# Layer 2's row ends with features on partitions and layer 3's weights centred beforehand

## The chip, the cores and the metric

The kernel runs on one core of one Trainium2 chip. The metric is the time of one execution in microseconds (us); the time before is 1886.3 us, the median of 4 runs (1885.71 to 1888.77). Engines are named as in the profile: PE is TensorE (PEld its weight loads), DVE is VectorE, ACT is ScalarE, POOL is GpSimd, SP is SyncE, whose queue issues most loads.

## The reference, cut to what matters

Four graph layers run over the same 2708 x 256 matrix `x` and the same 2708 x 2708 matrix `adj`. Each layer's output is added to its input and the rows are normalised. What the change touches is the end of layer 2 and the products that layer 3 begins with:

```python
# layer 2: GRU cells on 256 features; dn = de = diagonal of adj
y = dn[:, None] * (edge_output + node_output)          # layer 2's result
x = layernorm(x + y)                                   # (v - mean(v)) / sqrt(var(v) + 1e-5) by rows
# layer 3
h = x @ neigh_W.T
h = adj @ h / (adj.sum(axis=1, keepdims=True) + 1.0)
z = concatenate([x, h], axis=-1) @ lin_W.T
x = layernorm(x + z)
```

`neigh_W` is 256 x 256 and `lin_W` is 256 x 512. Since `adj @` acts from the left, the kernel uses `z = x @ A + (adj @ (x @ B)) / degree`, with A the first half of `lin_W.T` and B = `neigh_W.T` times its second half. A and B side by side, 256 x 512, are `lwn` in the code. So a finished row of layer 2 is needed for two products: `x @ A`, which is added to the row and kept in `y3_d` until layer 3 ends that row, and `x @ B`, the row of `h3` that layer 3 multiplies with `adj`.

## The kernel before, in words

Rows are cut into 22 tiles of 128 (the last has 20), `NT = 22`; 256 features are two chunks of 128 (`FC = 2`). A tile of rows can lie in memory with rows on partitions or, transposed, with features on partitions.

**Layer 0 and its preparation (to about 250 us).** While PE multiplies strips of `adj` with `x`, the weights of layer 3 are prepared in the pool `prep`: `lw` (`lin_W.T`) and `nw` are loaded by SP's queue, A is stored to `lwn_d` by POOL (L548), `nw` is transposed (L554), B is multiplied (L559), copied out by ACT (L562) and stored by POOL (L563). `lwn_d` is read back into `lwn` at the start of layer 2 (L373). In the same stage DVE picks out `diag`, the diagonal of `adj`, as a 128 x 22 table with rows on partitions (L458).

**Layer 1 (250 to 610 us) and the statistics of layer 2 (to some 720 us)** follow. At the end of the latter, small tables are transposed by PE (L966), copied by ACT (L970) and stored by POOL to `st_d` (L976).

**Layer 2's main loop (from about 890 us, L1247).** The 2708 columns are covered by three units, each with two halves of 512, 512 and 330 columns. For each unit and each of three heads, eleven steps run. One step loads blocks of `adj` by SP's queue (L264), builds two tiles `p` with two ACT instructions and one DVE product each (L1258 to L1262), makes four sums of them on DVE (L304 to L307), and issues seven PE products (`seven`, L317; a 32-bit product appears twice in the profile, so 14 there, a transpose once) into seven PSUM banks: `m1` takes one, `m26`, `m75` and `m43` two each. The eighth PSUM bank is `bank()`, a pool with a single buffer. Whoever takes it waits until what it held before has been read out.

**What is put between.** Everything else of layer 2 runs in slots between those products: `seven` calls `between()` after its third and its sixth product (`slots` = (2, 5); in the first unit of layer 3, after each product for some of the steps), and each call runs the next piece, up to a `yield`, of a generator from the lists `urgent` and `later`. `urgent` has `project` (L1098). `later` has `node(u, est)` of the unit before: for each half, the GRU cell (`cell`, L1115, products at L1128), whose result `yt` has features on partitions; the addition of the edge cell's result `et` (L1217); then the row ends. Layer 3 needs `h3` of all rows and so waits for the last unit's row ends (`while urgent or later: between()`, L1331).

**The row ends.** `by_tiles` (L1191) cuts a half into row tiles; a tile that lies in two halves is put together by POOL (L1201) and ended when its second part is there. Each tile takes three slots:

- `node_rows` (L1152): PE transposes the two chunks of `yt` into `bank` (L1157). DVE multiplies them by the rows' `diag` and adds the residual `xs[t]` (L1160). Then `layernorm` (L178): `bn_stats` (L170), `bn_aggr` (L172) and an addition (L174) on DVE, the power -0.5 on POOL (L175), and the normalisation on DVE (L181).
- `rows_turned` (L1166): PE transposes the normalised row back (L1170), ACT copies it out of `bank` (L1172).
- `rows_end` (L1175): PE multiplies its two chunks with `lwn` into one bank of 512 columns (L1179, four products of 512 columns in the profile). ACT copies the right half to `h3` (L1180), DVE adds the left half to the row (L1181), POOL stores the row to `y3_d` (L1182).

The loop in `node` (L1220) sets these apart: in step i it does `node_rows` of tile i, `rows_end` of tile i-2, `rows_turned` of tile i-1.

**What sets the order.** The program's order gives priorities; a scheduler in the compiler, which works with durations of its own, orders the instructions of each engine, and each engine then runs its own in that order and waits at the head of its queue. Buffers of a pool are reused when all who used them are done; `nleft` keeps one buffer of most tags (`xt2` and `et` for a cell's inputs, `yt` for its result), so the next half's inputs are loaded by POOL's queue (`load_cell`, L1184) when the cell before has let go of them.

The last function that the diff touches, for rows of `adj` with negative entries (`layer2_signed`, behind a branch that isn't taken with this data), ends its rows by `layer2_end` (L218).

## Time and profile before

| what | before |
| --- | --- |
| median of 4 runs | 1886.3 us (1885.71 to 1888.77) |
| the profiled execution | 1889.28 us |
| its span, first to last instruction | 1887.2 us |
| PE busy, instructions | 1843.2 us (98%), 7561 |
| DVE busy | 1279.8 us (68%), 2280 |
| ACT busy | 689.9 us (37%), 1419 |
| POOL busy | 254.9 us (14%), 419 |
| granted TensorE clock, mean | 0.996 |
| row ends of the first unit (two halves) | 1216 to 1291 and 1326 to 1375 us |
| row ends of the second unit | 1482 to 1525 and 1567 to 1609 us |
| row ends of the third unit | 1674 to 1692 and 1717 to 1741 us |

Busy time is summed over an engine's instructions; matmuls are pipelined, so their durations overlap and a busy PE isn't PE at its peak. A line of the timeline has start and length in us, engine, line of the kernel, operation, what is written and read, shapes and count; brackets at the end tell how long the engine had been idle and what ended that.

### The profile page before, as it was taken

To read this page: it belongs to the slowest core of one execution; us is meant where nothing else is said; L and a number is where in the kernel's file an instruction comes from. 1 tells how busy PE (TensorE), PEld (TensorE's weight loads), DVE (VectorE), ACT (ScalarE), POOL (GpSimd) and SP (SyncE) were. 2 spreads that over 40 slices of the span, in tenths; PEclk is the share of its full clock that TensorE was granted. 3 is DMA by queue.
4 is the path that set the end of the run, shared out by engine and by line. 5 is a ranking of instruction groups with operands and counts; after the bars stand their busy time and mean duration, and the time that the engine had idled before them with its cause. 6 is when DMAs were issued, how large, how long until landed. Compare 5 with 4: busy or idle time off the path is not lost.

```text
span 1887.2 us, 23114 instructions
## 1 busy us (share of the span) xinstructions
PE 1843.2 (98%) x7561; PEld 1037.0 (55%) x7565; DVE 1279.8 (68%) x2280; ACT 689.9 (37%) x1419; POOL 254.9 (14%) x419
## 2 busy tenths in 40 slices
PE   8999999999999999999899999999999999999997
PEld 6788842233345886887444444444445555654555
DVE  4344479998897655554667887785977758844664
ACT  3444410033244214111446655555564555311011
POOL 1211120001012311000001000110200201111111
PEclk9999999999999999999999999999999999999999
DMA  8344410100003657554647665454554445533764
GB/s 284 130 157 145 153 46 1 30 1 12 12 7 79 143 134 215 121 136 106 198 135 207 175 170 165 113 164 114 159 153 112 126 103 137 160 100 108 194 167 126
DMA packets 434205, 235.92 MB, mean 125 GB/s; under 512 B 184183, under 2 KB 421389, under 8 KB 431645
## 3 DMA queue, kind: packets, MB, share of 16 engines
q1 hardware_dynamic: 417438, 207.41, 39.9%
q0 software_dynamic: 7760, 21.20, 3.6%
q10 hardware_dynamic: 8878, 5.76, 1.0%
q8 instruction: 62, 1.02, 0.2%
q14 instruction: 67, 0.54, 0.1%
HBM read 221.61 MB, written 12.65 MB: 124 GB/s over the span
## 4 chain that ended last, share of the span: by engine, by line
PE 82%; DMA 6%; DVE 4%; issue 2%; ACT 2%; SPq 2%; POOL 1%; ACTq 0%; DVEq 0%; POOLq 0%
PE m L317 37%; PE acc L763 11%; PE bank L1128 7%; PE acc L211 7%; PE den L772 6%; PE gate L1003 4%; PE bank L1104 3%; DMA strip<-in_adj_t_dram 2%; SPq L264 2%; PE bank L1179 1%; ACT below L465 1%; PE pm L419 1%; DMA p<-in_adj_t_dram 1%; DVE p L1262 1%; POOL bn_rs L175 1%
## 5 line engine op out<-in xcount | busy, mean ns | idle before, releaser
L781 DVE SCALAR_TENSOR_TENSOR p<-fall_b,rise,mask 128x1024 f32<-128x1024 f32 (+1 forms) x264 | 293.6, 1155 | 32.8 <-PE den L772 16.7
L1258 ACT ACTIVATE p<-st,e_neg 128x1024 f32<-128x1024 f32 (+1 forms) x198 | 197.2, 1040 | 206.3 <-PE m L317 202.2
L317 PE MATMUL m<-s,xq 128*128 128x512 f32 (+3 forms) x660 | 230.1, 467 | 0.0
L763 PE MATMUL acc<-p,h 128*64 128x512 f32 (+2 forms) x1056 | 214.5, 548 | 0.2 <-ACT sum L794 0.2
L317 PE MATMUL m<-p,xq 128*128 128x512 f32 (+1 forms) x396 | 183.0, 544 | 0.5 <-DVE p L305 0.4
L211 PE MATMUL acc<-turn,strip 128*128 128x257 f32 x792 | 181.5, 379 | 0.0
L1261 ACT ACTIVATE p<-p 128x1024 f32<-128x1024 f32 (+1 forms) x198 | 178.8, 943 | 0.2
L317 PE MATMUL m<-p,x 128*128 128x512 f32 (+1 forms) x396 | 169.6, 547 | 5.1 <-DVE p L1262 4.8
L1262 DVE TENSOR_TENSOR p<-p,blk 128x1024 f32<-128x1024 f32 (+1 forms) x132 | 143.5, 1106 | 40.8 <-ACT p L1261 25.3
L317 PEld LDWEIGHTS m<-s,xq 128*128 128x128 f32 x660 | 124.3, 190 | 74.7 <-issue 57.7
L304 DVE TENSOR_TENSOR s<-p 128x512 f32<-128x512 f32 (+3 forms) x132 | 81.8, 621 | 119.8 <-PE m L317 98.2
L211 PEld LDWEIGHTS acc<-turn,strip 128*128 128x128 f32 x792 | 147.3, 190 | 20.3
L763 PEld LDWEIGHTS acc<-p,h 128*64 128x64 f32 x1056 | 69.8, 136 | 138.2 <-issue 128.6
L317 PE MATMUL m<-s,x 128*128 128x512 f32 (+3 forms) x330 | 127.4, 468 | 0.0
L317 PEld LDWEIGHTS m<-p,x 128*128 128x128 f32 x396 | 74.8, 191 | 79.3 <-issue 61.4
L772 PE MATMUL den<-p,h 128*32 128x512 f32 (+2 forms) x1056 | 117.7, 548 | 0.0
L317 PEld LDWEIGHTS m<-p,xq 128*128 128x128 f32 x396 | 74.4, 190 | 77.8 <-issue 60.5
L465 ACT ACTIVATE below<-strip 128x384 bf16<-128x384 f32 x132 | 78.4, 594 | 72.7 <-DMA strip<-in_adj_t_dram 69.3
L1262 DVE TENSOR_TENSOR p<-p,turn 128x1024 f32<-128x1024 f32 (+1 forms) x66 | 72.3, 1116 | 20.3 <-ACT p L1261 9.4
L305 DVE TENSOR_TENSOR p<-p 128x512 f32<-128x512 f32 (+3 forms) x132 | 81.8, 619 | 1.9
L317 PEld LDWEIGHTS m<-s,x 128*128 128x128 f32 x330 | 61.7, 190 | 38.4 <-issue 34.1
L307 DVE TENSOR_TENSOR s<-p,s 128x512 f32<-128x512 f32 (+3 forms) x132 | 81.1, 615 | 2.0
(276 smaller groups left out, 2536.3 us busy)
## 6 DMA issues: line engine op xcount, KB each, us to landing
strip<-in_adj_t_dram SPq DMA_DIRECT2D x19, 1408.0 KB, 6.0
blk<-in_adj_t_dram SPq DMA_DIRECT2D x88, 256.0 KB, 3.3
blk<-in_adj_t_dram SPq DMA_DIRECT2D x88, 192.0 KB, 3.9
pa<-in_adj_t_dram SPq DMA_DIRECT2D x110, 128.0 KB, 2.5
turn<-in_adj_t_dram SPq DMA_DIRECT2D x44, 256.0 KB, 3.1
blk<-in_adj_t_dram SPq DMA_DIRECT2D x88, 128.0 KB, 2.4
p<-in_adj_t_dram SPq DMA_DIRECT2D x88, 128.0 KB, 2.6
turn<-in_adj_t_dram SPq DMA_DIRECT2D x44, 192.0 KB, 3.2
```

The source lines that it names most:

```text
L211: nc.tensor.matmul(acc, s[:, c, :n], rhs(c), start=(c == 0), stop=(c == NT - 1))
L304: nc.vector.tensor_tensor(s1, a21, a22, ALU.add)
L305: nc.vector.tensor_tensor(a21, a21, a11, ALU.subtract)
L317: nc.tensor.matmul(dst[:, :w], lt, rt, start=start and not (one_bank and i), stop=stop and not (one_bank and i in (1, 2, 5)))
L465: nc.scalar.activation(below[:, : (hi - lo) * P], s[:, lo:hi].rearrange("p c n -> p (c n)"), AF.Relu, scale=-1.0, accum_out=negative[:, BE ...
L763: nc.tensor.matmul(acc[s][i * HD : (i + 1) * HD, :ws], hs[c][:, 2 * q + i, :HD], ps[i][:, p0 : p0 + ws], **flags,)
L772: nc.tensor.matmul(den[j : j + CT, :ws], hs[c][:, 2 * q + i, HD + 1 - CT :], ps[i][:, p0 : p0 + ws], **flags,)
L781: nc.vector.scalar_tensor_tensor(p[:, :w], falls[g // 2][:, 2 * q + i, :w], rise[:, c, 2 * q + i : 2 * q + i + 1], mask[:, c, at : at + w] ...
L1128: nc.tensor.matmul(g[:, :w], lt, rt, start=(q == 0), stop=(q == len(terms) - 1))
L1258: nc.scalar.activation(p[:, :, :w], st_k[:, :, :w], AF.Relu, scale=-1.0, bias=e_neg[:, at, k : k + 1])
L1261: nc.scalar.activation(p[:, :, :w], p[:, :, :w], AF.Exp, scale=-1.0)
L1262: nc.vector.tensor_tensor(p[:, :, :w], p[:, :, :w], blk[:, i, :, :w], ALU.mult)
```

## The change

Everything up to the normalisation is done with features on partitions, and the second transpose is left out.

1. The residual and the diagonal are applied to `yt` before it is transposed: two DVE instructions for a whole half, `yt * diag` and `yt + xt`. The diagonal is wanted along the free dimension, the same on all partitions: `diag` is transposed once, stored to `diag_d`, and each half loads its part, broadcast to 128 partitions, into `drow` by POOL's queue.
2. `node_rows` still transposes `yt` to have rows on partitions; ACT copies them out, and only the mean and the factor `rs` = (var + 1e-5)^-0.5 are computed there.
3. `rows_end` multiplies the rows as they were before the normalisation, straight from `yt`, with `lwn`. That (v - mean) * rs @ W = rs * (v @ Wc) holds if Wc is W with the mean over its 256 inputs taken off every column; `centred` does that once, in the preparation, with a matrix of -1/256. So ACT takes `h3` out of PSUM with the scale `rs`, and DVE takes the left half with `rs` and adds it to the row, which it has normalised.
4. The loop loses a slot for each tile: `node_rows` of tile i, `rows_end` of tile i-1.

```diff
+    diag_d = dram.tile([NT, P], F32, name="diag_d")
...
+                    minus = prep.tile([P, P], F32, name="minus")
+                    nc.gpsimd.memset(minus, -1.0 / F)
+
+                    def centred(w):
+                        pt = ps_t.tile([P, 4, P], F32, tag="tr", name="pt").rearrange("p i q -> p (i q)")
+                        for f in range(FC):
+                            nc.tensor.matmul(pt[:, :F], minus, w[:, f, :], start=(f == 0), stop=(f == FC - 1))
+                        nc.vector.tensor_tensor(w, w, pt[:, None, :F].to_broadcast([P, FC, F]), ALU.add)
+
+                    centred(lw[:, :FC])
                     nc.gpsimd.dma_start(lwn_d[:, :, :F], lw[:, :FC])
...
+                    centred(lwn2)
                     nc.gpsimd.dma_start(lwn_d[:, :, F:], lwn2)
...
+                pt = ps_t.tile([P, 4, P], F32, tag="tr", name="pd")
+                nc.tensor.transpose(pt[:NT, 0, :], diag, ident)
+                drows = tail.tile([NT, P], F32, name="drows", bufs=1)
+                nc.scalar.copy(drows, pt[:NT, 0, :])
+                nc.gpsimd.dma_start(diag_d, drows)
...
             y = nleft.tile([P, F], F32, tag="y", name="y", bufs=3)
-
-            nc.vector.scalar_tensor_tensor(
-                y[:n], pt[:n, :F], diag[:n, t : t + 1], xs[t][:n], ALU.mult, ALU.add,
-            )
-            layernorm(y, y, n)
-            return t, y
-
-        def rows_turned(t, y):
-            n = sz(t)
-            pt = bank()
-            for f in range(FC):
-                nc.tensor.transpose(pt[:, f * P : f * P + n], y[:n, f * P : (f + 1) * P], ident[:n, :n])
-            xt = nleft.tile([P, FC, P], F32, tag="xt", name="xt", bufs=2)
-            nc.scalar.copy(xt[:, :, :n], pt.rearrange("p (f q) -> p f q", q=P)[:, :FC, :n])
-            return t, y, xt
-
-        def rows_end(t, y, xt):
+            nc.scalar.copy(y[:n], pt[:n, :F])
+            mean, rs = moments(y, n)
+            return t, src, y, mean, rs
+
+        def rows_end(t, src, y, mean, rs):
+
             n = sz(t)
             pz = bank()
             for f in range(FC):
-                nc.tensor.matmul(pz[:n], xt[:, f, :n], lwn[:, f, :], start=(f == 0), stop=(f == FC - 1))
-            nc.scalar.copy(h3[t][:n], pz[:n, F:])
-            nc.vector.tensor_tensor(y[:n], y[:n], pz[:n, :F], ALU.add)
+                nc.tensor.matmul(pz[:n], src[:, f, :n], lwn[:, f, :], start=(f == 0), stop=(f == FC - 1))
+            nc.vector.tensor_scalar(y[:n], y[:n], mean, rs, ALU.subtract, ALU.mult)
+            nc.scalar.activation(h3[t][:n], pz[:n, F:], AF.Copy, scale=rs)
+            nc.vector.scalar_tensor_tensor(y[:n], pz[:n, :F], rs, y[:n], ALU.mult, ALU.add)
             nc.gpsimd.dma_start(y3_d[t], y[:n])
...
+        def load_diag(lo, w):
+
+            dst = nleft.tile([P, W], F32, tag="drow", name="drow")
+            src = bass.AP(tensor=diag_d.tensor, offset=diag_d.offset + lo, ap=[[0, P], [1, w]])
+            nc.gpsimd.dma_start(dst[:, :w], src)
+            return dst
...
                 xt, et = nxt or load_cell(lo, w)
+                drow = load_diag(lo, w)
                 yt = nleft.tile([P, FC, W], F32, tag="yt", name="yt")
                 yield from cell(est[h], xt, yt, w, *node_w, b_node)
                 nc.vector.tensor_tensor(yt[:, :, :w], yt[:, :, :w], et[:, :, :w], ALU.add)
+                nc.vector.tensor_tensor(
+                    yt[:, :, :w], yt[:, :, :w], drow[:, None, :w].to_broadcast([P, FC, w]), ALU.mult
+                )
+                nc.vector.tensor_tensor(yt[:, :, :w], yt[:, :, :w], xt[:, :, :w], ALU.add)
                 tiles = by_tiles(lo, w, lambda at, n: yt[:, :, at : at + n], shared)
-                got, turned = [], []
-                for i in range(len(tiles) + 2):
+                got = []
+                for i in range(len(tiles) + 1):
                     if i < len(tiles):
                         got.append(node_rows(*tiles[i]))
                         yield
-                    if i >= 2:
-                        rows_end(*turned[i - 2])
-                        yield
-                    if 0 < i <= len(tiles):
-                        turned.append(rows_turned(*got[i - 1]))
+                    if i:
+                        rows_end(*got[i - 1])
                         yield
```

## The prediction

> **What bounds the kernel now.** I read the page's busy line first, then the busy time by stage, then the timeline of TensorE (PE) and of VectorE (DVE) around one row end, and last what each of PE's row-end steps waits for. The row ends of layer 2 run between 1200 and 1762 us.
>
> ```profile
> PE 1843.2 (98%) x7561; PEld 1037.0 (55%) x7565; DVE 1279.8 (68%) x2280; ACT 689.9 (37%) x1419; POOL 254.9 (14%) x419
> ```
>
> ```profile
> 1200.00:1420.00 220.00, 217.60 (x527) 96.28 (x526) 169.52 (x237) 124.31 (x141) 32.91 (x43) 1.00 0.51 143
> 1420.00:1620.00 200.00, 195.09 (x626) 113.69 (x625) 148.96 (x291) 106.91 (x163) 26.89 (x45) 1.00 0.47 122
> 1620.00:1762.00 142.00, 138.53 (x431) 74.30 (x430) 84.67 (x201) 24.21 (x48) 23.53 (x42) 1.00 0.46 123
> ```
>
> The second view is by stage: length, then busy PE, weight loads, DVE, ACT, POOL, then clock, DMA share and GB/s. PE is busy 97 to 99% of all three stages at a clock of 1.00, DVE 60 to 77%, ACT 17 to 57%, DMA half. A busy PE is only modelled, so I also took the start of each matmul less the start of the one before and its pitch. The pitch is read from the timeline: four 512-column products take 1.72 us (1227.76 to 1229.48), 0.43 each; two 128-column transposes take 0.22 (1218.86 to 1219.08), 0.11 each. Between 1200 and 1765 us some 20 us are left as gaps; all else is PE issuing. So **PE's instruction count is the time here, and what is taken off it comes back one to one.**
>
> I call the three PE steps of a row tile N (transpose of the cell's result, L1157), T (transpose of the normalised row, L1170) and E (product with lwn, L1179).
>
> ```profile
> 1218.86 0.38 PE L1157 MATMUL bank<-ident,yt 128*128 128x128 f32 x2
> 1219.08 1.02 PE L317 MATMUL m<-p,x 128*128 128x512 f32 x2
> ...
> 1222.14 0.41 PE L1170 MATMUL bank<-ident,y 128*128 128x128 f32 x2 [0.32 <-DVE y L181]
> ...
> 1227.76 1.88 PE L1179 MATMUL bank<-lwn,xt 128*128 128x512 f32 x4
> 1229.48 1.88 PE L317 MATMUL m<-s,xq 128*128 128x512 f32 x4
> 1231.19 1.02 PE L317 MATMUL m<-p,xq 128*128 128x512 f32 x2
> 1232.92 0.44 PE L1170 MATMUL bank<-ident,y 128*128 128x128 f32 x2 [0.71 <-DVE y L1181]
> ```
>
> The reader is to see two kinds of wait. The T at 1222.14 waits for the normalisation (L181): its operand. The T at 1232.92 waits for L1181: E's result is still being read out of the only free PSUM bank. Of the gaps, T after N has 2.6 us (4 of them), T after E 4.6 (6), the first N of a half 2.7 (4), E after N 1.6 (4), and pairs inside a step 0.9.
>
> **The change part by part.**
>
> *T goes.* 22 tiles, two transposes each: 44 x 0.11 = 4.8 us of PE. With them go the waits for a normalised row, 2.6 us, and the 0.3 us inside the pairs. What is late next: the 4.6 us of T after E aren't T's, they belong to whatever takes the bank after E. Per half-unit of four tiles the order was N0 N1 T0 N2 E0 T1 N3 E1 T2 E2 T3 E3 (three T after an E) and becomes N0 N1 E0 N2 E1 N3 E2 E3 (three steps after an E). I keep the 4.6 whole. Its ends: all of it gone, or E's readout longer by the normalisation that now stands ahead of it on DVE (0.41, L181) in 18 places, 7.4 us more. I take 0, because L181 needs no bank and E's own products last 1.72 us.
>
> *N's readout* goes from DVE (L1160, 0.48) to an ACT copy (0.37, as L1172 had). E after N waited 1.6 us for L1160; the copy stands behind ACT's exponentials of 1.0 to 1.1 us (L1258, L1261) instead. Between -1.6 and +22 x 1.1 = +24 if every copy missed by one exponential; T's readout by the same copy cost the next step under 0.1 us in this trace, so I take 0.
>
> *h3 out of PSUM with a scale* on ACT: between the plain copy, 0.37 (L1180), and 0.60 (L1292, scale and bias), so 0 to 5 us over the kernel on an engine with 43% idle at its busiest. It holds the bank 0.2 longer at most; 0 taken. The scale comes through bn_stats, bn_aggr, the sum and POOL's power: N at 1224.11, power done at 1230.35, 6.2 us later. E stands two slots behind its N: 6.0 of layer products, 0.2 of N, 1.7 of its own, so its readout starts about 7.9 us after N. The slack is 1.7 us; if it is missed, ACT and DVE both queue behind the scale and the bank is held.
>
> ```profile
> 1224.10 1.21 DVE L1262 TENSOR_TENSOR p<-p,blk 128x1024 f32<-128x1024 f32 x1
> ```
>
> ```profile
> 1220.62 0.93 POOL L175 TENSOR_TENSOR bn_rs<-bn_rs,neg_half 128x1 f32<-128x1 f32 x1 [1.41 <-DVE bn_rs L174]
> 1224.26 1.46 POOL L175 TENSOR_TENSOR bn_rs<-bn_rs,neg_half 128x1 f32<-128x1 f32 x1 [2.72 <-DVE bn_rs L174]
> ```
>
> The power's median is 0.56 us, but beside a DVE product it took 1.46. The Trainium skill ("SBUF — State Buffer", Who interferes with whom) says that a DVE instruction with two SBUF inputs shuts out a GpSimd instruction that reads SBUF until it ends; these rows agree, and the rule speaks against this change, which adds 12 such DVE instructions. By it up to one power in each of six halves would be 0.9 us later, 5.4 us in all if nothing hid it; the sum goes without it, since the slack above covers 0.9.
>
> *Diagonal and residual on yt.* Six halves, two DVE instructions each. The row of the same shape is L1217: 1.22 us at 1024 elements (four halves), 0.85 at 660 (two); 2 x (4 x 1.22 + 2 x 0.85) = 13.2 us. A broadcast operand costs the same: L328 has one and takes 1.22. Off DVE go 22 x 0.48 (L1160), and L1181 (0.41) becomes an instruction like L1160: net +4.2 us of 1280. That DVE is not the bound shows here:
>
> ```profile
> 1215.53 1.22 DVE L1217 TENSOR_TENSOR yt<-yt,et 128x1024 f32<-128x1024 f32 x1
> 1216.66 0.69 DVE L306 TENSOR_TENSOR s<-s,p 128x512 f32<-128x512 f32 x1
> 1217.39 0.69 DVE L307 TENSOR_TENSOR s<-p,s 128x512 f32<-128x512 f32 x1
> ```
>
> L307 ends at 1218.08 and PE uses its s4 at 1224.33, 6.3 us later; in the narrow units, at 1482, 5.2. So 2.4 us more on DVE doesn't starve the products. It does delay N0, which reads yt: in this half PE took N0 at 1216.89, 0.14 after L1217. Bounds: 0 if the scheduler that orders the instructions moves N0 behind other products (it does move them: the N at 1218.86 stands inside a pair of a layer step, not at a slot), 13.2 if N0 stays. Nearest row: today's 2.7 us of N0 waits, behind a dependent chain of g_z 0.67, L1146 0.69, L1147 0.69, L1217 1.22 = 3.3 us. With 2.44 more the chain is 1.75 times as long, and I let the wait grow with it: +2.0.
>
> *Prologue.* Two calls of `centred` with two products each; a 32-bit product appears twice in the trace (four in the code at L559, eight there), so eight of 256 columns at 0.216 (L1358: 24 in 5.18 us) = 1.7 us of PE. PE has 7 us of gaps in 210 there, so it counts in full. The two DVE additions (some 0.7, as L306) lie under PE's strip products; without that cover 1.4 us, and POOL's store of lwn waits for them with the powers of three row tiles behind it. One transpose of diag: 0.1. Its store is one issue on POOL (0.5, L976) ahead of nine of the same kind; it is read some 450 us later.
>
> *Loads.* Six broadcast loads of the diagonal, at most 256 KB, issue 0.7 us each on POOL; the nearest row, st<-st of 512 KB, lands in 4.6 us, and the cell ahead of the first use lasts over 30. The next xt now waits for the addition of xt on DVE instead of the last product with whh (1209.60), so till about 1219; behind it on POOL stand et, which waited till 1217.05 anyway, and the first power, which follows N0. xt lands in 6.2 us, and the next cell starts at 1279.6, or two slotted steps (16 us) earlier with four slots fewer. 0.
>
> **Sum:** -4.8 - 2.6 - 0.3 + 2.0 + 1.7 + 0.1 = -3.9 us. The profiled execution took 1889.28 (span 1887.2 and 2.1 around it), 3.0 above the median of 1886.3; the sum is a difference and is taken from the median: **1882.4 us**.
>
> **Rivals.** Within 0.2% (3.8 us, about what a measurement of this kernel can tell) counts as no change.
> *The bank waits take the gain.* If every E is read out one normalisation late in half of its 18 places (+3.7), the result is -0.2: 1886.1. For it: the bank is single, and six T after E waited for just this. Against it: 1.7 us of slack.
> *N0 stays in its slot.* The mechanism is PE's order: N0 stands ahead of products that are ready, and waits 2.44 us (1.7 in the narrow halves) for the two new DVE instructions. Without its wait the sum is -5.9; -5.9 + 13.2 = +7.3: 1893.6, slower. It decides once N0's added wait is above 5.9 / 6 = 1.0 us per half (1.6, with 3.8 us more, to be measured as slower). For it: four of six N0 already wait, up to 1.1 us. Against it: N's are moved in this trace.
> *More than forecast.* With L1160 gone DVE reads E out sooner, and T after E (4.6) and E after N (1.6) shrink too: -3.9 - 6.2 = -10.1: 1876.2. For it: all ten of these waits end with a DVE instruction of the row ends (L1181, L1160). Against it: DVE gets 13.2 us of new work in just these stretches.
> That the change doesn't do what it says can only mean that PE wasn't the limit; the stage view speaks against that.
>
> **Chances.** Forecast 0.40, which lies at the bound of 3.8 us and goes half to faster (0.22, for N0's wait may be less than I let it grow) and half to the same (0.18); more than forecast 0.22; bank waits 0.16, the same; N0 in its slot 0.22, slower. That is 0.44 faster, 0.34 the same, 0.22 slower. The range runs from 1874 (just past the best case) to 1892 (most of the price of N0).
>
> **What would show it.** Right: no L1170; N0's wait at L1157 under 5 us in all; PE gaps between 1200 and 1762 of about 19 us; L1179's readers waiting seldom for POOL's power. Wrong: PE idle before L1157 by about 2 us per half (N0 rival), ACT idle at h3's copy with POOL's power as releaser (bank rival), or gaps ahead of L317 released by DVE, which would mean that DVE has become the bound.

## The result and the profile after

The changed kernel takes **1888.4 us** (median of 32 runs, 1886.0 to 1893.4) against 1885.7 for the kernel before (52 runs, 1884.0 to 1888.8): ratio 1.0015, 95% interval 1.001 to 1.002. That is 2.8 us slower (1.9 to 3.8), within the 0.2% (3.8 us) that the prediction counts as no change. 1882.4, 3.9 us faster, was predicted: the time moved the other way. The profiled execution took 1889.15 with a span of 1887.4, as long as that of before (1889.28 and 1887.2).

The page's busy line, and then the busy time by stage (length, busy PE, PEld, DVE, ACT, POOL, clock, DMA share, GB/s), of the changed kernel:

```profile
PE 1839.0 (97%) x7526; PEld 1034.4 (55%) x7530; DVE 1285.0 (68%) x2272; ACT 692.8 (37%) x1420; POOL 257.4 (14%) x427
```

```profile
1200.00:1420.00 220.00, 217.56 (x513) 94.67 (x512) 171.48 (x236) 124.81 (x143) 30.95 (x45) 1.00 0.52 147
1420.00:1620.00 200.00, 194.07 (x610) 113.30 (x609) 149.71 (x287) 106.37 (x162) 30.94 (x48) 0.99 0.47 122
1620.00:1762.00 142.00, 136.15 (x415) 73.00 (x415) 85.34 (x200) 24.28 (x48) 25.11 (x43) 1.00 0.48 126
```

PE has 35 instructions fewer (7561 to 7526: 44 transposes gone, nine products and transposes new in the preparation) and lost 4.2 us of modelled busy time (1843.2 to 1839.0); DVE gained 5.2 (4.2 were priced). But with less work PE doesn't end sooner: it is less busy in all three stages, and the clock of the middle one has dropped to 0.99. What PE waits for between 1200 and 1762 us (line waited for, in us, times, longest), before and after:

```profile
PE bank L1170 <- DVE y L1181: 3.6, 5, 1.0
PE bank L1170 <- DVE y L181: 1.9, 3, 1.2
...
PE bank L1157 <- POOL yt L1201: 1.3, 2, 1.0
PE bank L1179 <- DVE y L1160: 0.9, 3, 0.4
PE bank L1157 <- DVE yt L1217: 0.7, 2, 0.5
```

```profile
PE bank L1174 <- DVE y L1188: 5.4, 6, 1.8
PE bank L1174 <- POOL yt L1215: 4.2, 2, 3.8
PE bank L1185 <- DVE y L1188: 2.3, 4, 1.2
```

In the changed kernel N is L1174, E L1185, DVE's read of E L1188. T's wait for its row (L181) is gone, as foreseen. In its place the step after E waits longer for E's bank (5.4 + 2.3 against 3.6), and one first N of a half waits 3.8 us for POOL.

The same by the prediction's own measure (start of a product, less the start of the one before and its pitch; 1200 to 1765 us), with four experiments that are told below:

| gaps of PE, us | before | after | no additions | ACT reads E | POOL's copy on ACT | best version |
| --- | --- | --- | --- | --- | --- | --- |
| first N of a half | 2.7 | 5.0 | 2.9 | 4.4 | 0.8 | 0.4 |
| step after E | 4.6 | 9.9 | 3.6 | 0.5 | 10.0 | 0.2 |
| step after a later N | 4.3 | 0.6 | 0.0 | 1.7 | 0.4 | 0.5 |
| all | 20.1 | 25.5 | 14.7 | 15.9 | 20.2 | 9.1 |

The two places that grew can be read in the timeline. First the bank (start, length, engine, line, operation):

```profile
1220.09 1.88 PE L1185 MATMUL bank<-lwn,yt 128*128 128x512 f32 x4
...
1222.07 0.47 ACT L1187 ACTIVATE turn<-bank,bn_rs 128x256 f32<-128x256 f32 x1 [2.27 <-PE bank L1185]
...
1223.41 0.41 DVE L1186 TENSOR_SCALAR y<-y,bn_mv,bn_rs 128x256 f32<-128x256 f32 x1 [0.44 <-POOL bn_rs L176]
...
1223.74 1.22 DVE L1278 TENSOR_TENSOR p<-p,blk 128x1024 f32<-128x1024 f32 x1
1224.88 0.48 DVE L1188 SCALAR_TENSOR_TENSOR y<-bank,bn_rs,y 128x256 f32<-128x256 f32 x1
...
1225.41 0.44 PE L1174 MATMUL bank<-ident,yt 128*128 128x128 f32 x2 [0.87 <-DVE y L1188]
```

E's last product leaves PE at 1221.81. ACT reads its half at once, 0.47 us. DVE's half lies until 1224.88, 3.1 us after E, behind (among others) the next tile's normalisation, for whose scale DVE waits 0.44 us on POOL, and a product of 1.22 us. DVE takes its instructions in their order, and the read-out comes after these. The next N finds the only bank taken. Then POOL, in the third half:

```profile
1553.55 1.21 DVE L1233 TENSOR_TENSOR yt<-yt,drow 128x1024 f32<-128x1024 f32 x1
...
1554.73 3.85 POOL L276 TENSOR_TENSOR blk<-blk,offdiag 128x128 f32<-128x128 f32 x1 [0.46 <-issue]
1555.10 1.21 DVE L1236 TENSOR_TENSOR yt<-yt,xt 128x1024 f32<-128x1024 f32 x1
...
1558.52 0.76 POOL L247 DMA_DIRECT2D et<-edget  x1
1559.28 0.57 POOL L1202 DMA_DIRECT2D drow<-diag_d  x1
...
1560.03 0.53 POOL L1215 COPY yt<-yt 128x108 f32<-128x108 f32 x2
1560.36 0.68 PE L1174 MATMUL bank<-ident,yt 128*128 128x128 f32 x2 [3.80 <-POOL yt L1215]
```

The residual's addition (L1236) ends at 1556.31, but N starts at 1560.36, 4.05 us later: its tile is shared by two halves and is put together by POOL (L1215). POOL is held until 1558.58 by L276, which clears a block's own diagonal, and then issues two loads (1.3 us) and a short L276 ahead of the copy. L276 has a median of 0.45 us; here, beside a row of DVE instructions that read two SBUF tiles each, it took 3.85. After this wait the records of the granted clock show 0.5 for 3.41 us.

### The profile page after: what moved, and what is told of

Read it like the earlier page. It is cut to its first block, busy times and chain, and to the rows that moved or that the text cites. A ratio compares the mean times of both kernels' runs of the same rounds, so it can differ in the third digit from the quotient of the medians.

```text
span 1887.4 us, 23104 instructions
## 1 busy us (share of the span) xinstructions
PE 1839.0 (97%) x7526; PEld 1034.4 (55%) x7530; DVE 1285.0 (68%) x2272; ACT 692.8 (37%) x1420; POOL 257.4 (14%) x427
## 4 chain that ended last, share of the span: by engine, by line
PE 82%; DMA 5%; DVE 5%; issue 2%; ACT 2%; SPq 2%; POOL 1%; ACTq 0%; POOLq 0%; DVEq 0%
PE m L318 36%; PE acc L775 11%; PE acc L212 9%; PE bank L1145 8%; PE den L784 6%; PE gate L1020 4%; PE bank L1121 3%; SPq L265 2%; DVE p L1278 1%; PE pm L420 1%; DMA xt<-xt 1%; POOL bn_rs L176 1%; DMA p<-in_adj_t_dram 1%; PE bank L1185 1%; PE pq L941 1%
## 5 line engine op out<-in xcount | busy, mean ns | idle before, releaser
L318 PE MATMUL m<-s,xq 128*128 128x512 f32 (+3 forms) x660 | 230.6, 467 | 0.0
L318 PE MATMUL m<-p,xq 128*128 128x512 f32 (+1 forms) x396 | 183.0, 544 | 0.6 <-DVE p L306 0.4
L318 PE MATMUL m<-p,x 128*128 128x512 f32 (+1 forms) x396 | 171.0, 549 | 5.1 <-DVE p L1278 4.8
L318 PEld LDWEIGHTS m<-s,xq 128*128 128x128 f32 x660 | 124.6, 190 | 75.9 <-issue 58.4
L318 PE MATMUL m<-s,x 128*128 128x512 f32 (+3 forms) x330 | 127.7, 469 | 0.0
L318 PEld LDWEIGHTS m<-p,x 128*128 128x128 f32 x396 | 75.5, 193 | 80.8 <-issue 60.8
L318 PEld LDWEIGHTS m<-p,xq 128*128 128x128 f32 x396 | 74.2, 190 | 78.8 <-issue 62.1
L318 PEld LDWEIGHTS m<-s,x 128*128 128x128 f32 x330 | 62.5, 191 | 40.1 <-issue 35.8
```

What stands on the lines that cost most here:

```text
L318: nc.tensor.matmul(dst[:, :w], lt, rt, start=start and not (one_bank and i), stop=stop and not (one_bank and i in (1, 2, 5)))
```

## The experiments

Theory A: the two new DVE instructions, and POOL behind them, delay the first N. Theory B: they put DVE behind, and E's bank, which DVE reads, comes free late. (In the first four expectations B still is narrower: the bank's two readers come one after the other, or the normalisation stands ahead of DVE's.) Each run was timed against the kernel before in five rounds; us are the ratio less one times 1886.

| run | ratio (95%) | us against before |
| --- | --- | --- |
| changed kernel | 1.0015 (1.0010 to 1.0020) | +2.8 |
| e1 no additions | 0.9954 (0.9940 to 0.9967) | -8.7 |
| e2 normalisation early | 1.0021 (1.0011 to 1.0031) | +4.0 |
| e3 only T gone | 0.9964 (0.9951 to 0.9978) | -6.8 |
| e4 additions by chunk | 0.9998 (0.9989 to 1.0008) | -0.4 |
| e5 ACT reads E | 0.9950 (0.9937 to 0.9964) | -9.4 |
| e6 e4 and e5 | 0.9935 (0.9921 to 0.9948) | -12.3 |
| e7 before + additions | 1.0027 (1.0018 to 1.0036) | +5.1 |
| e8 before + prologue | 1.0008 (0.9998 to 1.0017) | +1.5 |
| e9 additions beside the path | 1.0008 (0.9999 to 1.0017) | +1.5 |
| e10 e5, no additions | 0.9937 (0.9923 to 0.9950) | -11.9 |
| e11 before, ACT reads E | 1.0014 (1.0005 to 1.0023) | +2.6 |
| e12 e6, POOL relieved | 0.9919 (0.9906 to 0.9933) | -15.3 |
| e13 e1 with the loads | 0.9956 (0.9942 to 0.9969) | -8.3 |
| e14 e1, N read by DVE | 0.9963 (0.9949 to 0.9976) | -7.0 |
| e15 POOL relieved | 0.9982 (0.9973 to 0.9991) | -3.4 |
| e16 its copy alone | 0.9994 (0.9985 to 1.0003) | -1.1 |
| e17 its load alone | 1.0012 (1.0003 to 1.0021) | +2.3 |
| e18 e1, copy on ACT | 0.9946 (0.9932 to 0.9960) | -10.2 |

### The parts by themselves: e3, e8, e7, e1, e13

e3, the kernel before without T:

```diff
-        def rows_turned(t, y):
...
-                nc.tensor.matmul(pz[:n], xt[:, f, :n], lwn[:, f, :], start=(f == 0), stop=(f == FC - 1))
+                nc.tensor.matmul(pz[:n], src[:, f, :n], lwn[:, f, :], start=(f == 0), stop=(f == FC - 1))
```

> The kernel before with the second transpose and its copy taken away: E multiplies the cell's own columns (so the normalisation, diagonal and residual are missing from what E multiplies), one step of two slots less per tile as in the changed kernel, E read out as before by an unscaled copy and an addition, nothing new between cell and N. This is the price of T alone. Prediction's terms: 4.8 of transposes, 2.6 of waits for the normalised row, 0.3 in pairs: 7.7 us under the kernel before, with the 4.6 of waits after E kept. Theory A expects just that, 1878. Theory B expects the waits after E to grow here too, since it is then E and not T that stands after E: 2 to 5 us under the kernel before.

Measured -6.8 us: the prediction's 7.7 lies in the interval (4.1 to 9.2). PE's gaps after E were 5.4 us, 0.9 more than before. T was worth about what was said. Of the longer waits after E that theory B expected here, these 0.9 are all.

e8, the kernel before with `centred` and its two calls:

```diff
+                    centred(lw[:, :FC])
...
+                    centred(lwn2)
```

> The kernel before with the weights centred in the prologue and nothing else (the rows that they meet have mean zero, so the result is the same): the price of the prologue alone. The prediction's term was 1.7 us, all on PE. Rival: the prologue's PE waits for loads at that point, and the eight products lie in those waits: 0 to 0.5 us.

+1.5 (-0.4 to 3.2): the forecast of 1.7 fits; nothing at all isn't excluded.

e7, the kernel before with two more DVE instructions in the place of the new ones:

```diff
                 nc.vector.tensor_tensor(yt[:, :, :w], yt[:, :, :w], et[:, :, :w], ALU.add)
+                nc.vector.tensor_tensor(yt[:, :, :w], yt[:, :, :w], et[:, :, :w], ALU.mult)
+                nc.vector.tensor_tensor(yt[:, :, :w], yt[:, :, :w], xt[:, :, :w], ALU.add)
```

> The kernel before, its second transpose and all else kept, with two more DVE instructions per half between the cell and the first N: yt multiplied by et and then added to xt (the computation is changed by that: yt is not the reference's here; the shapes and costs on DVE are those of the change, 13.2 us in six halves). This is the price of the new DVE work alone. The prediction's term was 2.0 (bounds 0 and 13.2). Theory B: DVE falls behind by 2.4 us per half, the T after E and N's read-out come later, and with the first N's wait the price is 7 to 11 us, 1894 to 1898. Theory A: the first N's wait and perhaps a stretch at half clock, 2 to 5 us, 1889 to 1892.

+5.1, between the two theories' ranges. The place tells more: the first N waits 2.3 us, less than before (2.7), while E after N, which waits for DVE's read of N's bank (L1160), goes from 0.9 to 4.2 in the view of waits. PE's gaps are 25.7 in all, 5.6 more. The price is paid at the bank.

e1, the changed kernel without the additions and the load; in e13 the first line of the diff stays:

```diff
-                drow = load_diag(lo, w)
...
                 nc.vector.tensor_tensor(yt[:, :, :w], yt[:, :, :w], et[:, :, :w], ALU.add)
-                nc.vector.tensor_tensor(
-                    yt[:, :, :w], yt[:, :, :w], drow[:, None, :w].to_broadcast([P, FC, w]), ALU.mult
-                )
-                nc.vector.tensor_tensor(yt[:, :, :w], yt[:, :, :w], xt[:, :, :w], ALU.add)
```

> The changed kernel without the diagonal's product, the residual's sum and the load of the diagonal (these three are left out of what is computed); everything else stands. It takes away what stands new between the cell and the first N of a half. Theory A (the first N waits for the two new DVE instructions, PE pauses, and a pause of some 4 us costs a stretch at half clock): PE's wait at the first N falls from 5.0 us back to 2.7 or less, no half-clock stretch near 1560, about 3.5 to 5 us less than the changed kernel, so 2 us under the kernel before. Theory B (E's bank is held by its two readers one after the other): the steps after E keep their 10 us of waits, and the time is within 1 us of the changed kernel. If both hold, the first N's waits go and the waits after E stay.

> The changed kernel without the diagonal's product and the residual's sum (left out of what is computed), but with the six loads of the diagonal still issued on POOL. Its twin without the loads took 8.7 us less than the kernel before. If the 11.5 us that separate that twin from the changed kernel are DVE's work, the loads alone cost 0 to 1 us: 1878 to 1880. If POOL's queue ahead of the shared tile's copy and the powers is part of it, 2 to 4 us: 1881 to 1883.

e1 -8.7, e13 -8.3: the six loads cost nothing that shows here (0.4, intervals overlap), and the two DVE instructions per half cost **11.5 us** with them, 11.1 without: nearly all of DVE's 13.2, and more than either theory had for e1. Both theories' places give way. What PE waited for in e1:

```profile
PE bank L1174 <- DVE y L1188: 1.5, 1, 1.5
PE bank L1174 <- POOL yt L1215: 1.3, 2, 1.0
PE bank L1185 <- DVE y L1188: 0.9, 2, 0.5
```

The waits for DVE's read of E fell from 7.7 to 2.4, those for POOL's copy from 4.2 to 1.3.

### Delay or bank: e9, e4, e2, e5, e10, e11, e14

e9 keeps DVE's load but takes it off the first N's path; the two instructions behind the addition of `et` go, and these come:

```diff
                         got.append(node_rows(*tiles[i]))
+                        if i == 0:
+                            nc.vector.tensor_tensor(
+                                et[:, :, :w], et[:, :, :w], drow[:, None, :w].to_broadcast([P, FC, w]), ALU.mult
+                            )
+                            nc.vector.tensor_tensor(et[:, :, :w], et[:, :, :w], xt[:, :, :w], ALU.add)
```

> The changed kernel with the same two DVE instructions per half, of the same shapes, made on the tile et after it has been added and behind the first N of the half, so that nothing waits for their result (the residual and the diagonal are missing from what N turns; the load of the diagonal stays). DVE's load is that of the changed kernel, but the first N's operand comes 2.4 us earlier. Without these instructions the kernel took 8.7 us less than the kernel before, with them 2.8 more: 11.5 us are to be split. Theory A (delay of the first N's operand): most of the 11.5 goes, 1879 to 1881, N0's waits 3 us, and the waits after E fall too. Theory B (DVE's load ahead of E's read-out): most stays, the waits after E stay at 8 to 10 us, 1885 to 1888.

+1.5 (1889.3): of the 11.5 only 1.3 went. That speaks for B, but not cleanly. The edit made a wait of its own, in one half (timeline):

```profile
1483.65 0.59 POOL L1202 DMA_DIRECT2D drow<-diag_d  x1 [5.37 <-DVE et L1239]
...
1489.19 0.47 ACT L1187 ACTIVATE turn<-bank,bn_rs 128x256 f32<-128x256 f32 x1 [4.53 <-POOL bn_rs L176]
...
1491.69 0.69 PE L1174 MATMUL bank<-ident,yt 128*128 128x128 f32 x2 [2.95 <-DVE y L1188]
```

POOL's next load of the diagonal waits for the moved DVE instruction; the power of `rs` stands behind it, and behind a load that waits for PE next; ACT and DVE wait for the scale, and N for the bank. So some 3 us of what stayed are e9's own.

e4 does the three steps for each chunk of features, inside the cell:

```diff
+                def finished(j):
+                    a = yt[:, j, :w]
+                    nc.vector.tensor_tensor(a, a, et[:, j, :w], ALU.add)
+                    nc.vector.tensor_tensor(a, a, drow[:, :w], ALU.mult)
+                    nc.vector.tensor_tensor(a, a, xt[:, j, :w], ALU.add)
...
```

> The changed kernel with the addition of et, the product with the diagonal and the addition of xt made for one chunk of features at a time, each as soon as the cell has finished that chunk; the result is the same. Half of this work then lies under the cell's second chunk, and only three DVE instructions of about 0.69 us (512 columns) stand between the cell's end and the first N, in place of three of 1.21. Theory A: the waits of the first N fall from 5.0 to about 3 us and the stretch at half clock near 1560 goes: 2 to 4 us less than the changed kernel. Theory B: within 1 us of the changed kernel.

-0.4, 3.2 less than the changed kernel. The first N's gaps fell to 3.1 (from 5.0), but the gaps after E fell as well, to 7.4 (from 9.9), so the run doesn't part the theories; a stretch at half clock stayed, at 1557.

e2 moves a row's normalisation, in the program, from E's read-out to N:

```diff
             mean, rs = moments(y, n)
+            nc.vector.tensor_scalar(y[:n], y[:n], mean, rs, ALU.subtract, ALU.mult)
             return t, src, y, mean, rs
...
-            nc.vector.tensor_scalar(y[:n], y[:n], mean, rs, ALU.subtract, ALU.mult)
```

> The changed kernel with the normalisation of a row moved from rows_end into node_rows, straight after its moments, so that it no longer stands ahead of E's read-out on DVE; the result is the same. Theory A: no change against the changed kernel (within 1 us), N0's waits as they were. Theory B in the form that the prediction gave it (0.41 us of normalisation ahead of the read-out in up to 18 places): the steps after E wait up to 7 us less, and the time falls by 3 to 7 us. Theory B in another form (the scaled copy on ACT first, then DVE, one after the other): waits after E stay near 10 us and the time stays within 1 us.

+4.0, no better than the changed kernel (+2.8, intervals overlap), with 10.2 us of gaps after E. But on DVE the normalisation didn't get out of the way (timeline; E is L1186 here, the normalisation L1178):

```profile
1218.49 1.88 PE L1186 MATMUL bank<-lwn,yt 128*128 128x512 f32 x4
...
1223.02 0.41 DVE L1178 TENSOR_SCALAR y<-y,bn_mv,bn_rs 128x256 f32<-128x256 f32 x1 [0.44 <-POOL bn_rs L176]
1223.35 0.48 DVE L1188 SCALAR_TENSOR_TENSOR y<-bank,bn_rs,y 128x256 f32<-128x256 f32 x1
```

The next tile's normalisation, and DVE's wait for its scale, stand right ahead of the read-out, which again starts 3.1 us after E (PE left it at 1220.21). In 14 of the 22 read-outs a normalisation starts between E's end and the start of DVE's read, as many as in the changed kernel. So e2 doesn't test the normalisation, on which the prediction's first rival rested; that rival stays open. The changed kernel's trace speaks for a part of it. Every normalisation there finds DVE waiting for POOL:

```profile
L1186 DVE TENSOR_SCALAR y<-y,bn_mv,bn_rs 128x256 f32<-128x256 f32 (+1 forms) x22 | 9.1, 412 | 13.0 <-POOL bn_rs L176 13.0
```

The 13.0 us are nothing new (12.8 before, 12.6 in e1), but 9.2 of them fall between E's end and DVE's read, against 5.8 in e1 and 4.3 before. From E's end to DVE's read it is 35.6 us in all 22, against 28.4 in e1 and 30.9 before. What of it PE would be spared without the normalisation in between, no run shows.

e5 takes DVE off E's bank, and with it all that stands ahead of the read-out in DVE's queue:

```diff
+            e = nleft.tile([P, W], F32, tag="drow", name="e")[:, :F]
             nc.scalar.activation(h3[t][:n], pz[:n, F:], AF.Copy, scale=rs)
-            nc.vector.scalar_tensor_tensor(y[:n], pz[:n, :F], rs, y[:n], ALU.mult, ALU.add)
+            nc.scalar.activation(e[:n], pz[:n, :F], AF.Copy, scale=rs)
+            nc.vector.tensor_tensor(y[:n], y[:n], e[:n], ALU.add)
```

> The changed kernel with E read out of its bank by ACT alone: the scaled copy of h3 and a second scaled copy of the other half into SBUF; DVE then adds that copy to the normalised row, off the bank. Same result, DVE has as many instructions as before, ACT 22 more of about 0.47 us. Theory B, sharpened by the runs so far (ACT's read starts 0.26 us after E, but DVE's read stands behind one or two of DVE's products of 1.2 us and starts up to 3.1 us after E, longest in the halves where the two new additions have put DVE behind): the bank is free some 1.4 us after E, inside the 1.7 us of the next four products; the waits of N after E (6.7) and E after E (3.2) fall to 2 us or less in all; time 6 to 8 us under the changed kernel, about 1881. Theory A (only the first N's chain matters): waits after E fall but the time stays within 2 us, 1887 or more. A third theory, ACT's own queue: its exponentials of 1.0 to 1.1 us stand ahead of the second copy and the waits after E stay above 6 us.

-9.4: **12.2 us less than the changed kernel**, by one more ACT instruction and one more pass over 256 columns. The gaps after E fell from 9.9 to 0.5; the first N still has 4.4. Its timeline at the place shown above:

```profile
1224.38 1.88 PE L1185 MATMUL bank<-lwn,yt 128*128 128x512 f32 x4
...
1226.36 0.47 ACT L1188 ACTIVATE turn<-bank,bn_rs 128x256 f32<-128x256 f32 x1 [2.27 <-PE bank L1185]
...
1226.73 0.47 ACT L1189 ACTIVATE e<-bank,bn_rs 128x256 f32<-128x256 f32 x1
...
1227.81 0.38 PE L1174 MATMUL bank<-ident,yt 128*128 128x128 f32 x2
1228.03 1.22 DVE L1280 TENSOR_TENSOR p<-p,blk 128x1024 f32<-128x1024 f32 x1
...
1229.16 0.42 DVE L1190 TENSOR_TENSOR y<-y,e 128x256 f32<-128x256 f32 x1
```

DVE is as late as before, its addition comes 3.1 us after E (PE left it at 1226.10), behind the same product of 1.22. But the bank was free at 1227.20, and N started without a wait.

e10 is e5 without the additions and the load.

> The kernel in which ACT alone reads E, once more without the diagonal's product, the residual's sum and the diagonal's load (these are left out of what is computed). Together with its twin that has them (9 us under the kernel before) it prices the two additions where DVE no longer reads E's bank. If the 11.5 us that they cost with DVE's read-out were mostly E's bank (theory B), they cost only the first N's wait here, 2 to 4 us: 1875 to 1877. If they cost through the first N (theory A) they cost 8 us or more here too: 1871 or less.

-11.9: with ACT as E's reader the additions cost 2.5 us (intervals overlap), with DVE as its reader 11.5. This settles where most of their price is paid: not in DVE's time, not at the first N, but at the bank behind DVE's queue. Which of the instructions in that queue (products, sums, normalisations with their waits for POOL) holds the bank for how much isn't parted.

e11 puts the same reader into the kernel before:

```diff
+            e = xt.rearrange("p f q -> p (f q)")
             nc.scalar.copy(h3[t][:n], pz[:n, F:])
-            nc.vector.tensor_tensor(y[:n], y[:n], pz[:n, :F], ALU.add)
+            nc.scalar.copy(e[:n], pz[:n, :F])
+            nc.vector.tensor_tensor(y[:n], y[:n], e[:n], ALU.add)
```

> The kernel before with E read out by ACT alone: a second plain copy, into the tile xt, which E has finished with, and DVE's addition from there; same result. It asks whether the read-out's gain needs the change at all. Theory B: the T after E waits of 4.6 us go to 1 or less, 3 to 4 us under the kernel before, and so less than the 12 us that the same edit gave in the changed kernel, since the old order has a T and its slack between E and the next N. Rival: the second copy stands behind ACT's exponentials and the time stays within 1 us.

+2.6: no gain, the theory missed. The wait of T after E did fall (gaps 4.6 to 0.9), but the bank has another DVE reader there, N's (L1160), and the wait went to it. What PE waits for in e11:

```profile
PE bank L1179 <- DVE y L1160: 3.7, 5, 2.2
PE bank L1170 <- DVE y L181: 1.9, 3, 1.2
```

3.7 against 0.9 before. PE's gaps are the same in sum (20.0 and 20.1), so why the kernel is 2.6 us slower stays open. ACT's read-out of E pays only together with the change. That it does so because the change has given N's read-out to ACT is read from this wait; no run parts the two in the changed order.

e14 asks how much that was worth, in e1's kernel:

```diff
-            nc.scalar.copy(y[:n], pt[:n, :F])
+            nc.vector.tensor_copy(y[:n], pt[:n, :F])
```

> The changed kernel without the two additions and the load (left out of what is computed), with N read out of its bank by a plain DVE copy in place of ACT's. Theory B says that any reader of the bank on DVE stands behind DVE's products: N's bank comes free later, E after N waits again (1.6 us and more in the kernel before), and the time rises by 2 to 5 us over the twin with ACT's copy (8.7 under the kernel before), to 1880 to 1884. Rival: N's reader has slack, since E follows two slots later, no change within 1 us: 1878.

-7.0 against -8.7: 1.7 us, with intervals that overlap; not shown.

### POOL: e15, e16, e17, e18

e15 is both edits, e16 the second alone, e17 the first alone; e18 is the second in e1's kernel.

```diff
-            nc.gpsimd.dma_start(dst[:, :w], src)
+            nc.sync.dma_start(dst[:, :w], src)
...
-                    nc.gpsimd.tensor_copy(ends[t][:, :, c0:c1], got)
+                    nc.scalar.copy(ends[t][:, :, c0:c1], got)
```

> The changed kernel with the load of the diagonal on SP's queue and the shared tile's copy on ACT; same result. In its trace one first N waits 3.8 us for POOL's copy and a stretch at half clock follows. If that is worth what it looks like, 3 to 5 us less than the changed kernel: 1884 to 1886. If the wait goes back to DVE's additions, which end just before, or to the bank, within 1 us of the changed kernel: 1888 to 1890.

> The changed kernel with the copy of a tile that two halves share on ACT in place of POOL, and nothing else; same result. If the first N that waited 3.8 us for this copy waited because POOL was held by an instruction drawn out to 3.85 us beside DVE's additions, this edit alone gives nearly all of the 6 us that the relief of POOL gave: 1882 to 1884. If the load's issue ahead of the copy was the cause, it gives 1 to 2 us.

> The changed kernel with the load of the diagonal issued on SP's queue in place of POOL's, and nothing else; same result. The load cost nothing where the additions were left out. If that holds here, the time stays within 1 us of the changed kernel, 1888 to 1890; if its 0.57 us of issue ahead of the shared tile's copy counts, 1 to 2 us less.

> The changed kernel without the two additions and the load (left out of what is computed), with the shared tile's copy on ACT. The kernel without the additions took 8.7 us less than the kernel before and still had 2.9 us of waits at the first N, 1.3 of them put down to POOL's copy. If the relief belongs to the additions, it gives 1 to 2 us here against 6 with them: 1876 to 1878. If the copy on POOL costs as much without them, 1873 or less.

Against the changed kernel: both -6.2, the copy -3.9, the load -0.5 (none). Nearly all of the 6.2 was expected of the copy; the intervals of both and of the copy alone overlap. In e18 the copy gives 1.5 over e1 (intervals overlap). So the additions cost 11.5 with the copy on POOL and 9.1 (e16 less e18) with it on ACT; that difference is within the intervals. In e15's timeline POOL is held just as long, and N doesn't care:

```profile
1555.59 4.12 POOL L276 TENSOR_TENSOR blk<-blk,offdiag 128x128 f32<-128x128 f32 x1 [0.19 <-DMA blk<-in_adj_t_dram]
...
1556.23 1.21 DVE L1236 TENSOR_TENSOR yt<-yt,xt 128x1024 f32<-128x1024 f32 x1
1557.47 0.50 ACT L1215 COPY yt<-yt 128x108 f32<-128x108 f32 x2 [0.76 <-DVE yt L1236]
...
1557.81 0.44 PE L1174 MATMUL bank<-ident,yt 128*128 128x128 f32 x2
```

N starts 0.37 us after L1236 ends, in place of 4.05, and no stretch at half clock follows.

### A version that beats both: e6, e12

> The changed kernel with both edits: E read out by ACT alone, and the additions and the diagonal's product made chunk by chunk inside the cell. Same result. If A and B each hold a part and add up: 2 us (chunks) and 6 to 8 us (read-out) under the changed kernel, 1878 to 1880, which is faster than the kernel before. If the read-out alone carries it: the same as with the read-out alone, within 1 us.

> The kernel with ACT's read-out and the work by chunks (12 us under the kernel before), with POOL relieved of two more things: the load of the diagonal goes to SP's queue and the copy of a tile that two halves share to ACT. Same result. If POOL's queue holds up the first N of some halves (2.5 us of waits are left there), up to 2 us less, 1873 to 1875. If those waits are the chain on DVE and not POOL, no change; ACT's copies can also hold up a read-out: up to 1 us more.

e6 -12.3, e12 **1872.3 us, -15.3** (ratio 0.9919, 0.9906 to 0.9933): e5, e4 and e15 together. The gains by themselves (12.2, 3.2 and 6.2 against the changed kernel) sum to 21.6, together they give 18.1. Its busy time by stage, first two lines:

```profile
1200.00:1420.00 220.00, 220.00 (x522) 96.83 (x521) 172.52 (x243) 129.17 (x153) 29.77 (x41) 1.00 0.53 148
1420.00:1620.00 200.00, 199.95 (x644) 119.11 (x644) 159.02 (x316) 113.47 (x176) 36.13 (x56) 1.00 0.50 130
```

In these two stages busy PE is at 100%, with DVE busier than in the changed kernel; in the third it is 140.16 of 142. By the starts of products, which aren't modelled, 9.1 us of the 25.5 are left.

## Why the prediction was wrong

**T goes (-4.8, -2.6, -0.3): right.** 7.7 against 6.8 measured (e3), and the waits that stand after E then were kept nearly whole in e3, 5.4 against 4.6.

**Prologue (+1.7): not refuted**, 1.5 (e8, -0.4 to 3.2). **Loads (0): right** within the intervals, 0.4 (e13 less e1).

**Diagonal and residual on yt (+2.0): the step that failed.** It measured 11.5, near the upper bound of 13.2. The sentence "2.4 us more on DVE doesn't starve the products" was true: the longest waits of L318 between 1200 and 1762 us end with a DMA (1.5 us), none with DVE. But the delay was then looked for at one reader only, the first N. There it added 2.3 us of gaps, near the 2.0 by luck: 4.0 of the 5.0 are the one wait for POOL at 1560, and the other first N of a half wait 1.0 us in all (1.6 before), though DVE's chain ahead of them is longer. The step left out two more places where the new instructions are paid: E's bank, whose release waits in DVE's queue (gaps after E 9.9 against 3.6 in e1), and POOL, whose copy came late (4.2 against 1.3).

**"I keep the 4.6 whole": failed with it.** The gaps after E are 9.9, and the upper end of +7.4 allowed for these 5.3 more. It was turned down "because L181 needs no bank". The normalisation needs none, but it stands in the same queue as the read-out, with DVE's wait for its scale, and so do products of 1.22 us; how much is whose isn't parted. The slack of 1.7 us for the scale was mis-sized too: the schedule put E 2.2 us behind its own N in the first half (1217.87 and 1220.09), not two slots, and the scale was ready at 1221.87, 0.06 after E's end. For ACT it was just in time: of the 32.0 us that ACT idled before L1187, POOL ended 3.1. DVE waited for POOL before each of its 22 normalisations.

**N's readout and h3's scale on ACT (0): not refuted.** The gaps after a later N fell from 4.3 to 0.6, most of it T's own wait; e14 puts 1.7 us on N's reader, which its interval doesn't show. The scaled copy takes 0.47 for 0.37 and lies in the chain of two readers of E's bank: DVE's read never starts sooner than 0.75 us after E, in the kernel before 0.60.

**The rule on DVE and POOL.** The Trainium skill's "SBUF — State Buffer", Who interferes with whom, was weighed in the prediction for the powers and left out, as slack covered 0.9 us. The trace agrees with the rule at another instruction: L276's longest time is 3.85 us with the additions in a row (3.7 to 4.2 in e2, e5, e15 to e17), 1.5 in e1 and 1.4 before. It was 1.6 in e7, which has them in a row too, so the place counts as well. The powers, for which the rule was weighed, didn't get longer (longest 0.94 us between 1200 and 1765, 1.51 before). That the additions held L276 is inferred from their place; that the copy behind it cost 3.9 us is measured (e16).

**Does it add up?** T -6.8, prologue +1.5 and additions +11.5 give +6.2; +2.8 was measured. N's reader on ACT may give 1.7 of the 3.4; the rest is within the intervals, each some 2 us to either side. The gaps add up better: 5.4 us more of them (20.1 to 25.5), 4.8 of transposes less and 1.8 of preparation more, both as priced, give +2.4.

**The rivals.** "Bank waits take the gain" named the place and came nearest (1886.1); its mechanism, a normalisation ahead of the read-out, is in the trace, but its share is not shown. "N0 stays in its slot" had the price of the additions nearly right by luck, at the wrong place: N0's gaps were 5.0, not 13.2. Of the signs listed, no L1170 came true, N0's wait stood on its bound of 5 us, and PE's gaps were 25.5, not 19.

## What to carry to other kernels

An instruction that is added to an engine with 25% of its time to spare isn't paid by that engine's share of busy time, but by whatever stands behind it in its queue: look for every instruction there that frees something scarce, here the read-out of the one free PSUM bank. Count what these instructions wait for too: an instruction that waits for another engine's result holds up all that stand behind it. Let the engine with the shortest queue read such a bank, even at an extra pass (0.47 us more on ACT for each of 22 tiles saved 12 us here), but check that no other reader of the same bank stays on the late engine, or the wait only moves there. Before two-operand DVE products are put in a row, look what POOL has to do just then, and who waits for it.

## What the runs showed of the hardware

A pause of PE costs more than its length when the clock falls: the records of the granted clock show 0.5 for 3.41 us (twice that at some places) from about its end, and in e2's four products of E start 0.85 us apart at 1683 in place of 0.43. It did so in the middle of a kernel after gaps (by the starts, as in the table) of 1.8 (e7, at 1734), 2.1 (e5, at 955), 2.4 and 4.0 (e2), 2.7 (e4), 3.1 (e9) and 3.4 us (e5, e17), and not after others of 2.0 (changed kernel, at 1683), 2.1 (e6), 2.3 (e9, at 1561) and 2.4 us (e11, at 1583). The Trainium skill ("TensorE: Matmul & The Clock Gate", Why this matters for your kernels) asks for no idle gap of PE over some 3 us; here shorter ones were enough, though not always.
